# Four places in a two-layer decoder: the order of the first loads, of decay attention's first group, of the last softmax copies and of the last banks

## The chip, the cores and the metric

The kernel runs on one core of a Trainium2 chip. A core has five engines that run side by side and meet at semaphores: TensorE (PE: matmuls, and transposes as matmuls), VectorE (DVE), ScalarE (ACT), GpSimd (POOL) and SyncE (SP), which mostly issues transfers. ACT and POOL can issue transfers as well; SP and ACT have a queue each. Matmuls write to PSUM, which is divided into banks of 128 x 512 float32; DVE and ACT read results from there into SBUF. All other data lies in SBUF or in the chip's memory (HBM).

The metric is the device time of one execution, in microseconds (us); lower is better. Three runs are shown, and their median counts.

## The reference

The input is x, 16 sequences ("blocks" below) of 128 tokens of width 512. Two layers follow, with three sublayers each, and a layer norm behind each addition:

```python
x = _layernorm(x + _L0_attn_ref(x, ...))           # softmax attention, 16 heads, 4 kv heads
x = _layernorm(x + _L0_xattn_ref(x, ctx_512, ...)) # cross attention through latent weights
x = _layernorm(x + _L0_ffn_ref(x, w1, w2, w3))     # gated, ternary weights
x = _layernorm(x + _L1_attn_ref(x, ...))           # decay ("lightning") attention
x = _layernorm(x + _L1_xattn_ref(x, ctx_512, ...)) # softmax attention on the context
x = _layernorm(x + _L1_ffn_ref(x, ...))            # 8 experts, 2 per token, and a shared one
```

The first attention and the fourth sublayer are the ones that the change reaches first:

```python
# _L0_attn_ref
q = q * cos_q + _rotate_half(q) * sin_q
k = k * cos_k + _rotate_half(k) * sin_k
scores = jnp.einsum('btkgd,bskd->bkgts', qg, k) * scale
scores = scores + mask[None, None, None]
p = jax.nn.softmax(scores, axis=-1)
out = jnp.einsum('bkgts,bskd->btkgd', p, v).reshape(B, T, C)
return out @ wo.T + bo

# _L1_attn_ref, in chunks
scores = jnp.einsum('bhid,bhjd->bhij', qb, kb) * intra_decay[None]
o_intra = jnp.einsum('bhij,bhjd->bhid', scores, vb)
...
return out @ Wout + bout
```

The last sublayer adds, for each token, two experts weighted by a softmax gate and a shared expert:

```python
act = jax.nn.silu(gu[..., :F]) * gu[..., F:]
y = jnp.einsum('tef,te,ehf->th', act, combine, down_weights)
sact = jax.nn.silu(sgu[:, :Fs]) * sgu[:, Fs:]
y = y + sact @ shared_down.T
```

Everything is float32.

## The kernel before

All 16 blocks of x stay in SBUF, one tile of 128 tokens x 512 for each. Blocks are worked in four groups of four (`GB` = 4, `NG` = 4): the projections of a group work on 512 tokens at a time. The instructions are written in program order for all engines at once, and a scheduler of the framework then orders each engine's list by what is ready in its model; some instructions are tied to program order (`tc.keep_in_program_order`). Each engine runs its list strictly in order. PSUM's eight banks are shared out by tags (`psum.share`): in softmax attention two are called `mm`, four `sc` and two `pt`; in the last sublayer two `mm`, three `sc`, two `pt` and one `av`.

**The start.** SP's queue loads the rotary tables `rsn` and `rc`, then the weight `w` in five slices (L363) with the small `cols` and `bv` between, then `bo`, `wo` and x4 to x15. ACT's queue loads x0 to x3 (L358) and, after x0, `wv`. POOL multiplies w's halves by the sine table (`t`, L377), DVE multiplies w by the cosine table (L380) and adds the two (`wr`, L381), so that the rotation is in the weight. PE transposes x0 to x3 (L128), works out their values (`pv`, L462) and the 40 matmuls of `pq` (L165), then the first scores (`sc`, L488). POOL adds the output bias `bo` to each block of x (L448) before it comes to the softmax.

**Softmax attention.** `attend` is used by the first attention and by the fifth sublayer. In step n it works out the scores of block n, the values of block n-2 and the output projection of block n-2 (`project_out`, L176). In between, for each of four banks of scores: DVE adds the mask and takes the maximum (L212, L214), ACT takes the exponentials (L219), POOL divides by the sum (`finish`, L226), and `turn` transposes four heads' probabilities on PE into a `pt` bank (L231) and copies them to SBUF on DVE (`pT`, L233). The values (`av`, L494 and L1040) use these copies. A planner (`Share`) deals projections of the next group out over the steps; for block 15 (n = `NB`) in the second use none are left.

**Decay attention.** For each group: eight projections `pq` (L868), then four values `pv` (L878), which DVE copies with their bias to `v` (L883). Then each block goes into a `Pipeline` with lags 0, 1 and 2: its scores on PE (L901, with the decay multiplied in by DVE, `sT`, L908), one step later its values (L916, copied by ACT to `oT`, L921), and one step later its projection (L176). Scores use four `sc` banks, one set. The next group's blocks are transposed through HBM: `send4` copies a block to `xp` on ACT (L144), sends it to HBM (L145) and fetches it turned (L151), and `back` transposes 32 x 32 pieces on DVE (L154). There is one `xp` buffer, and there are two for fetched blocks.

**The end.** Experts' results are added to `sums` in HBM by indirect transfers. Then SP loads the 16 blocks of `sums` (L1392). Half of the shared expert's down projections are still to be done: three pairs of blocks, (8, 12), (9, 13) and (10, 14), by `shared_pair`, with 20 matmuls (L1326, two passes each included) and four short ones (L1334), and blocks 11 and 15 singly by `shared_down`. DVE adds each result to the loaded sum (L1411), in program order. The early blocks 0 to 7 lie between the pairs: POOL adds their sums (L1420). Statistics (L1429), a power on POOL (L1401), ACT's scaling (L1405) and the output transfer (L1408) follow for each.

Of the kernel before, what the change touches and what calls it, by code (L numbers as in the profile page):

```python
# [12 lines left out]
F32 = mybir.dt.float32  # L13
# [5 lines left out]
P = 128  # L19
NB = 16  # L20
D = 512
KC = D // P
# [24 lines left out]
def decoder_kernel(ctx: ExitStack, tc: tile.TileContext, a: dict, out: bass.AP):  # L47
    nc = tc.nc
# [153 lines left out]
    class Softmax:  # L202
# [22 lines left out]
            nc.vector.reciprocal(rs, self.sm)  # L225
            nc.gpsimd.tensor_tensor(self.p, self.p, spread(rs, P), ALU.mult)  # L226

        def turn(self):
            pt = bank("pt", [P, 4, P], "pt")
            for j in range(4):  # L230
                nc.tensor.transpose(pt[:, j, :], self.p[:, j, :], ident)  # L231
            self.pT = self.pool.tile([P, 4, P], F32, tag="pT", name="pT", bufs=4)
            nc.vector.tensor_copy(self.pT, pt)  # L233

    class Share:

# [18 lines left out]
    def attend(pool, mask, wo, prepare, score, value):  # L255


        held = {}
        share = Share(prepare(0), 1)
        share.deal()  # L260
        late = []
        for n in range(NB + 2):
            if n % GB == 0 and n < NB:
                share.rest()
                share = Share(prepare(n // GB + 1), 3 * GB if n + GB < NB else 3 * GB + 6)
            if n < NB:
                sc = [bank("sc", [P, 4, P], "sc") for _ in range(4)]
                score(sc, n)
                held[n] = [Softmax(pool, sc[c], mask) for c in range(4)]
            if n >= 2:  # L270
                av = bank("pt", [P, KC, P], "av")
                value(av, n - 2, [s.pT for s in held.pop(n - 2)])
                oT = pool.tile([P, KC, P], F32, tag="oT", name="oT")
                nc.scalar.copy(oT, av)
            for c in range(4):
                if n < NB:
                    held[n][c].start()
                    late.append(held[n][c])
                if late and (len(late) > 1 or n >= NB):
                    late.pop(0).finish()  # L280
                if 1 <= n <= NB:
                    held[n - 1][c].turn()
                if c == 1 and n >= 2:
                    project_out(oT, wo, n - 2)
                else:
                    share.deal()


    GB = 4
    TG = GB * P  # L290
# [48 lines left out]
    with tc.tile_pool(name="p1", bufs=1) as p1:  # L339
# [9 lines left out]

        with tc.tile_pool(name="p1a", bufs=1, side="right") as p1a:  # L350

            rsn = p1a.tile([P, 640], F32, tag="rsn", name="rsn")
            nc.sync.dma_start(rsn, a["rope_s"].partition_broadcast(P))
            rc = p1a.tile([P, 640], F32, tag="rc", name="rc")
            nc.sync.dma_start(rc, a["rope_c"].partition_broadcast(P))
            w = p1a.tile([P, KC, 640], F32, tag="w", name="w")
            for b in range(GB):
                nc.scalar.dma_start(x[b], a["x"][b])  # L358
                if b == 0:
                    nc.scalar.dma_start(wv, a["l0a_wqkv"][:, :, 640:768])  # L360
            for c in range(5):
                at = slice(c * P, (c + 1) * P)
                nc.sync.dma_start(w[:, :, at], a["l0a_wqkv"][:, :, at])  # L363
                if c == 0:
                    nc.sync.dma_start(cols, a["l0a_cols"])
                    nc.sync.dma_start(bv, a["l0a_bv"].partition_broadcast(P))
            mask1 = load_const("mask1", [P, P], a["mask_add"], p1)
            nc.sync.dma_start(bo, a["l0a_bo"].partition_broadcast(P))
            nc.sync.dma_start(wo, a["l0a_wo"])
            halves = "p (h t d) -> p h t d"  # L370
            for c in range(5):
                at = slice(c * P, (c + 1) * P)
                t1 = p1a.tile([P, KC, 4, 2, 16], F32, tag="t1", name="t1", bufs=2)
                w5 = w[:, :, at].rearrange("p k (h t d) -> p k h t d", t=2, d=16)
                s4 = rsn[:, at].rearrange(halves, t=2, d=16)
                for t in range(2):
                    nc.gpsimd.tensor_tensor(  # L377
                        t1[:, :, :, t, :], w5[:, :, :, 1 - t, :], bc4(s4[:, :, t, :], KC), ALU.mult
                    )
                nc.vector.tensor_tensor(wr[:, :, at], w[:, :, at], bc(rc[:, at], KC), ALU.mult)  # L380
                nc.vector.tensor_tensor(  # L381
                    wr[:, :, at], wr[:, :, at], t1.rearrange("p k h t d -> p k (h t d)"), ALU.add
                )
                if c == 0:
                    nc.vector.tensor_tensor(br, cols[:, 0, :], cols[:, 2, :], ALU.mult)
                    nc.vector.tensor_tensor(b2, cols[:, 1, :], cols[:, 3, :], ALU.mult)
                    nc.vector.tensor_tensor(br, br, b2, ALU.add)
# [423 lines left out]
    with tc.tile_pool(name="p4", bufs=1) as p4:  # L811
# [39 lines left out]
        for g in range(NG):  # L851
# [20 lines left out]
                if c in (2, 4) and g + 1 < NG:  # L872
                    send4((g + 1) * GB + c // 2 - 1)
            vs = []
            for i in range(GB):
                pv = bank("mm", [P, D], "pv")
                for k in range(KC):
                    nc.tensor.matmul(  # L878
                        pv, lhsT=xT[:, k, i * P : (i + 1) * P], rhs=wq4[k // 2][:, k % 2, 2 * D : 3 * D],
                        start=(k == 0), stop=(k == KC - 1),  # L880
                    )
                v = p4.tile([P, D], F32, tag="v", name="v", bufs=6)
                nc.vector.tensor_tensor(v, pv, bv4, ALU.add)  # L883
                vs.append(v)
            if g + 1 < NG:
                xT = p4.tile([P, KC, TG], F32, tag="xT", name="xT")
            for i in range(GB):
                if i in (0, 2) and g + 1 < NG:
                    for n in (i, i + 1):
                        coming.pop(0).back(xT[:, :, n * P : (n + 1) * P])  # L890
                        if i == 0:
                            send4((g + 1) * GB + 2 + n)
                toks = slice(i * P, (i + 1) * P)
                mine = {}

# [26 lines left out]
                    mine["oT"] = oT  # L922

                pipe.push((scores, values, lambda mine=mine, b=g * GB + i: project_out(mine["oT"], wo4, b)))
        pipe.drain()
    pre_pool.__exit__(None, None, None)

# [126 lines left out]
    with tc.tile_pool(name="p6", bufs=1, reuse_waits="tile") as p6:  # L1054
# [173 lines left out]
        with tc.tile_pool(name="p6r", bufs=1, side="right", reuse_waits="tile") as p6r:  # L1228
# [85 lines left out]
                    lambda po: then(b, po),  # L1314
                )

            def shared_pair(tasks, pair, then):


                got = {}  # L1320
# [1 line left out]
                def whole(b, m_):  # L1322
                    g, i = divmod(b, GB)
                    if m_ == 0:
                        got[b] = bank("mm", [P, D], "po")
                    nc.tensor.matmul(  # L1326
                        got[b], lhsT=acts[g][:, m_, i * P : (i + 1) * P], rhs=sw_dn[:, m_, :],
                        start=(m_ == 0), stop=False,
                    )
# [84 lines left out]
            for blocks in order:  # L1414
                tasks = []
                if blocks[0] >= EARLY and len(blocks) == 2:
                    shared_pair(tasks, blocks, add_late)
                for b in blocks:
                    if b < EARLY:
                        tc.keep_in_program_order(nc.gpsimd.tensor_tensor(x[b], x[b], ys[b], ALU.add))  # L1420
# [143 lines left out]
```

## Time and profile before

| what | value |
|---|---|
| median of three runs | 2063.01 us (2058.14 to 2064.41) |
| the profiled execution | 2059.38 us |
| its span, first to last instruction | 2057.5 us |
| granted TensorE clock, mean | 0.992 |
| PE busy | 2006.5 us, 98% |
| DVE, ACT, POOL busy | 886.6, 627.7, 647.5 us |
| HBM read, written | 185.88, 75.83 MB |

A line of a timeline gives the start, the duration, the engine, the line of the kernel, the operation, what it writes from what, the shape and, after x, how many instructions are put together. In brackets behind it stand the idle time of the engine before it and what ended that. A line of the chain of waits gives the start, the duration and the work that the end waited for at that time. The granted clock is a share of full speed.

### The profile page before, as it was taken

What the parts mean: (1) busy time and instruction counts of PE and PEld (TensorE: products, weight loads), DVE (VectorE), ACT (ScalarE), POOL (GpSimd) and SP (SyncE); (2) the same over time, 40 slices, a digit from 0 to 9 for tenths busy, and PEclk for the clock granted to TensorE, in tenths of its full rate; (3) what the DMA queues carried; (4) which work ended last, traced back from release to release, by engine and by line L of the source; (5) the groups of instructions that cost most, each with busy time, mean ns of one, the idle gap of its engine ahead of it and who ended that gap; (6) DMA issues with size and microseconds to landing.
All of it is one profiled execution on the core that took longest, in us unless ns stands there. A gap on an engine that the chain in (4) does not pass through costs nothing.

```text
span 2057.5 us, 25359 instructions
## 1 busy us (share of the span) xinstructions
PE 2006.5 (98%) x9045; PEld 1110.9 (54%) x9045; DVE 886.6 (43%) x1775; ACT 627.7 (31%) x2107; POOL 647.5 (31%) x674
## 2 busy tenths in 40 slices
PE   8999999999999999999999999999899999999997
PEld 4555554444444468888554444555544455555552
DVE  4777732445554354342134414777731123233234
ACT  3555532333333333222311012766522200000002
POOL 7445520211222122223422113455613212323223
PEclk9999999999999999999999999999999999999999
DMA  9201241535432241001410018500013246786844
GB/s 250 87 17 40 104 143 56 158 118 174 149 124 91 71 121 60 16 11 62 147 42 21 11 41 265 203 22 22 27 61 116 95 133 185 226 247 192 264 89 169
DMA packets 164110, 227.87 MB, mean 111 GB/s; under 512 B 50576, under 2 KB 117520, under 8 KB 159248
## 3 DMA queue, kind: packets, MB, share of 16 engines
q1 hardware_dynamic: 149088, 152.80, 23.9%
q0 software_dynamic: 13792, 72.14, 11.6%
q8 instruction: 72, 1.18, 0.2%
q10 hardware_dynamic: 1104, 1.31, 0.2%
q14 instruction: 54, 0.44, 0.1%
HBM read 185.88 MB, written 75.83 MB: 127 GB/s over the span
## 4 chain that ended last, share of the span: by engine, by line
PE 84%; DMA 6%; DVE 3%; POOL 2%; issue 2%; ACT 1%; SPq 0%; POOLq 0%; DVEq 0%; ACTq 0%
PE po L649 10%; PE po L176 7%; PE pq L590 5%; PE pq L868 5%; PE pq L165 5%; PE pg L1143 4%; PE po L799 4%; PE pa L772 4%; PE pb L772 4%; PE pu L1143 3%; DMA sums<-ry,place 3%; PE ry L1292 3%; PE rg L1271 3%; PE ru L1271 3%; PE pv L878 3%; PE av L637 3%
## 5 line engine op out<-in xcount | busy, mean ns | idle before, releaser
L226 POOL TENSOR_TENSOR p<-p,rs 128x512 f32<-128x512 f32 x192 | 201.0, 1048 | 456.9 <-DVE rs L225 447.6
L649 PE MATMUL po<-mT,cc 128*128 128x512 f32 x512 | 230.4, 598 | 1.4 <-ACT cc L642 1.4
L219 ACT ACTIVATE p<-t,nmx 128x128 f32<-128x128 f32 x512 | 198.6, 390 | 33.8 <-POOL p L226 10.2
L649 PEld LDWEIGHTS po<-mT,cc 128*128 128x128 f32 x512 | 94.7, 190 | 115.0 <-issue 106.0
L219 ACT ACTIVATE p<-sc,nmx 128x128 f32<-128x128 f32 x256 | 90.3, 374 | 109.1 <-DVE nmx L214 93.8
L1241 POOL DMA_INDIRECT ew<-in_l1f_w_dram,which x39 | 40.6, 1042 | 246.6 <-PE ry L1292 167.2
L176 PE MATMUL po<-wo,oT 128*128 128x512 f32 x256 | 116.9, 600 | 0.4 <-ACT qkT L454 0.4
L590 PE MATMUL pq<-xT,wqr 128*128 128x512 f32 x256 | 115.8, 593 | 0.9 <-ACT xT L129 0.9
L1276 ACT ACTIVATE rsg<-rg 128x352 f32<-128x352 f32 x39 | 18.1, 464 | 320.6 <-PE rg L1271 297.0
L115 POOL TENSOR_SCALAR ve<-mv 128x1 f32<-128x1 f32 x80 | 17.8, 223 | 301.4 <-DVE mv L113 282.9
L868 PE MATMUL pq<-xT,wq 128*128 128x512 f32 x256 | 110.6, 592 | 0.7 <-ACT xT L129 0.7
L1292 PE MATMUL ry<-ew,ractT 128*128 128x512 f32 (+1 forms) x234 | 106.9, 592 | 0.0
L1271 PE MATMUL rg<-ew,xsT 128*128 128x352 f32 x312 | 100.1, 463 | 6.6 <-DMA ew<-in_l1f_w_dram,which 6.5
L122 POOL TENSOR_SCALAR x<-x,mv,rstd 128x512 f32<-128x512 f32 x48 | 100.5, 2094 | 4.5
L1271 PE MATMUL ru<-ew,xsT 128*128 128x352 f32 x312 | 98.7, 459 | 0.0
L219 ACT ACTIVATION_READ_ACCUMULATOR p<-t,nmx 128x1 f32 x512 | 96.3, 188 | 0.0
L233 DVE COPY pT<-pt 128x512 f32<-128x512 f32 x128 | 86.6, 679 | 19.4 <-PE pt L231 19.4
L783 POOL TENSOR_TENSOR hl<-ht,hh 128x512 fp32r<-128x512 f32 x44 | 57.4, 1305 | 108.1 <-ACT hh L781 108.1
L231 PEld LDWEIGHTS pt<-ident,p 128*128 128x128 f32 x512 | 60.6, 143 | 55.5 <-issue 41.5
L1143 PE MATMUL pg<-xT,sw_gu 128*128 128x512 f32 x192 | 86.5, 593 | 0.0
L1304 POOL DMA_INDIRECT sums<-ry,place x39 | 61.8, 1585 | 70.4 <-DMA sums<-ry,place 34.7
L214 DVE TENSOR_REDUCE nmx<-t 128x4 f32<-128x512 f32 x128 | 83.6, 676 | 0.8
(243 smaller groups left out, 3612.4 us busy)
## 6 DMA issues: line engine op xcount, KB each, us to landing
piece<-in_l0f_w_dram SPq DMA_DIRECT2D x48, 352.0 KB
away<-sq SPq DMA_DIRECT2D x32, 512.0 KB
pT<-away SPq DMA_DIRECT2D x128, 128.0 KB
raw<-in_l0x_raw_dram SPq DMA_DIRECT2D x8, 1728.0 KB
x<-turned SPq DMA_DIRECT2D x176, 64.0 KB
slots_x<-zero SPq DMA_DIRECT2D x1, 10023.0 KB
sums<-zero SPq DMA_DIRECT2D x1, 9984.0 KB
xs<-slots_x SPq DMA_DIRECT2D x156, 64.0 KB
```

The lines of the kernel that those rows point to most:

```text
L122: engine.tensor_scalar(x[b], x[b], mean, rstd, ALU.subtract, ALU.mult)
L165: nc.tensor.matmul(got["p"], lhsT=lhsT, rhs=rhs, start=(n == 0), stop=(n == len(pairs) - 1))
L176: nc.tensor.matmul(po, lhsT=oT[:, c, :], rhs=wo[:, c, :], start=(c == 0), stop=(c == KC - 1))
L219: nc.scalar.activation(self.p[:, j, :], src[:, j, :], AF.Exp, bias=nmx[:, j : j + 1], accum_out=self.sm[:, j : j + 1])
L226: nc.gpsimd.tensor_tensor(self.p, self.p, spread(rs, P), ALU.mult)
L590: nc.tensor.matmul(pq, lhsT=wqr[:, k, cols], rhs=xT[:, k, :], start=(k == 0), stop=(k == KC - 1))
L649: nc.tensor.matmul(self.po, lhsT=self.cc[:, 4 * par + j, :], rhs=mT[h], start=(par == 0 and j == 0), stop=(par == 1 and j == 3),)
L772: nc.tensor.matmul(dst, lhsT=wt[:, k, f * P : (f + 1) * P], rhs=xs[n][:, k, :], start=(k == 0 and n == 0), stop=(k == KC - 1 and n == 1),)
L868: nc.tensor.matmul(pq, lhsT=wq4[k // 2][:, k % 2, c * P : (c + 1) * P], rhs=xT[:, k, :], start=(k == 0), stop=(k == KC - 1))
L1143: nc.tensor.matmul(dst, lhsT=sw_gu[:, k, at : at + P], rhs=xTs[g][:, k, :], start=(k == 0), stop=(k == KC - 1),)
L1271: nc.tensor.matmul(dst, lhsT=self.xT[:, k, :], rhs=gu[:, k, off : off + FE], start=(k == 0), stop=(k == KC - 1),)
L1292: nc.tensor.matmul(po, lhsT=self.actT[:mw, m_, :], rhs=dn[:mw, m_, :], start=(m_ == 0), stop=(m_ == 2))
```

## The change

1. x1 and x3 are loaded by SP, ahead of everything else in its queue; x0, `wv` and x2 stay with ACT.
2. `turn` is told who copies. In step n = `NB` (block 15), in both uses of `attend`, the copies of the second and fourth bank (c = 1, 3) are ACT's; all others stay with DVE.
3. In decay attention's first group, the values and the attention of the blocks are interleaved: after `pv` of block 1, block 0 enters the pipeline, after `pv` of block 2, block 1. Blocks 2 and 3 follow after all four values, and the transposes for the next group (`back`) with the sends of blocks 6 and 7 come ahead of block 2. The other groups keep their order.
4. The pair (9, 13) takes the two `pt` banks in place of the `mm` banks.

The scheduler's order follows: DVE finishes `wr`'s first slice before it starts on the others, POOL makes all ten `t` products before its first addition of `bo`, and SP sends nine blocks in a row (L145) before it fetches blocks 6 and 7, where it sent seven.

```diff
-        def turn(self):
+        def turn(self, copy):
             pt = bank("pt", [P, 4, P], "pt")
...
-            nc.vector.tensor_copy(self.pT, pt)
+            copy(self.pT, pt)
...
-                    held[n - 1][c].turn()
+                    held[n - 1][c].turn(nc.scalar.copy if n == NB and c % 2 else nc.vector.tensor_copy)
...
+            for b in range(1, GB, 2):
+                nc.sync.dma_start(x[b], a["x"][b])
             rsn = p1a.tile([P, 640], F32, tag="rsn", name="rsn")
...
-            for b in range(GB):
+            for b in range(0, GB, 2):
                 nc.scalar.dma_start(x[b], a["x"][b])
...
-            for i in range(GB):
+            def values_in(i):
                 pv = bank("mm", [P, D], "pv")
...
-            if g + 1 < NG:
-                xT = p4.tile([P, KC, TG], F32, tag="xT", name="xT")
-            for i in range(GB):
-                if i in (0, 2) and g + 1 < NG:
-                    for n in (i, i + 1):
-                        coming.pop(0).back(xT[:, :, n * P : (n + 1) * P])
-                        if i == 0:
-                            send4((g + 1) * GB + 2 + n)
+            def attend_block(i):
                 toks = slice(i * P, (i + 1) * P)
...
+            began = 0
+            for i in range(GB):
+                values_in(i)
+                if g == 0 and 0 < i < GB - 1:
+                    attend_block(began)
+                    began += 1
+            if g + 1 < NG:
+                xT = p4.tile([P, KC, TG], F32, tag="xT", name="xT")
+            for i in range(GB):
+                if i in (0, 2) and g + 1 < NG:
+                    for n in (i, i + 1):
+                        coming.pop(0).back(xT[:, :, n * P : (n + 1) * P])
+                        if i == 0:
+                            send4((g + 1) * GB + 2 + n)
+                if i >= began:
+                    attend_block(i)
...
-            def shared_pair(tasks, pair, then):
+            def shared_pair(tasks, pair, then, tag="mm"):
...
-                        got[b] = bank("mm", [P, D], "po")
+                        got[b] = bank(tag, [P, D], "po")
...
-                    shared_pair(tasks, blocks, add_late)
+                    shared_pair(tasks, blocks, add_late, ("mm", "pt")[blocks[0] % 2])
```

## The prediction

> **What bounds the kernel now.** I read the page first, then the chain of waits, then the timeline of TensorE (PE) at the four places that the change touches, then the granted clock there. The page says that PE is busy nearly all the time, so only PE's own idle time, and time at a low clock, can be won:
>
> ```profile
> span 2057.5 us, 25359 instructions
> PE 2006.5 (98%) x9045; PEld 1110.9 (54%) x9045; DVE 886.6 (43%) x1775; ACT 627.7 (31%) x2107; POOL 647.5 (31%) x674
> ```
>
> Place 1, the first 43 us, in the chain of waits (start, duration, what). The reader is to see that GpSimd (POOL) holds PE up: it adds `bo` to 15 blocks, then normalizes the first probabilities, and only then does PE transpose them.
>
> ```profile
> 20.47 2.28 POOL t L377 x2
> 22.75 18.82 POOL x L448 x15
> 41.57 1.01 POOL p L226
> 42.62 0.69 PE pt L231 x2
> ```
>
> Place 2, PE's timeline where decay attention begins, and the same two operations one group later. Between the start of the first scores (1031.45) and the first projection (1043.13) lie 11.68 us; one group later, a score step and a value step follow each other without a wait.
>
> ```profile
> 1031.45 1.17 PE L901 MATMUL sc<-qkT 32*128 32x128 f32 x32
> 1034.09 3.87 PE L901 MATMUL sc<-qkT 32*128 32x128 f32 x32 [1.47 <-DVE sT L908]
> 1037.88 1.94 PE L916 MATMUL av<-sT,v 128*32 128x128 f32 x32
> 1039.75 2.44 PE L901 MATMUL sc<-qkT 32*128 32x128 f32 x32
> ...
> 1093.71 1.17 PE L901 MATMUL sc<-qkT 32*128 32x128 f32 x32
> 1094.81 1.08 PE L916 MATMUL av<-sT,v 128*32 128x128 f32 x32
> ```
>
> Place 3, the last block of the second softmax attention: PE waits for two copies that VectorE (DVE) makes one after the other.
>
> ```profile
> 1478.86 1.04 PE L231 MATMUL pt<-ident,p 128*128 128x128 f32 x8
> 1480.40 0.42 PE L1040 MATMUL av<-pT,v 128*32 128x128 f32 x6 [0.51 <-DVE pT L233]
> 1481.59 1.06 PE L1040 MATMUL av<-pT,v 128*32 128x128 f32 x26 [0.77 <-DVE pT L233]
> ```
>
> Place 4, the end: each late pair of blocks waits for DVE to read the banks of the pair before.
>
> ```profile
> 2010.59 1.13 PE L1334 MATMUL po<-sw_dn,half 64*128 64x512 f32 x4
> 2013.91 10.55 PE L1326 MATMUL po<-sw_dn,act 128*128 128x512 f32 x20 [2.19 <-DVE x L1411]
> ...
> 2026.29 8.85 PE L1326 MATMUL po<-sw_dn,act 128*128 128x512 f32 x20 [0.77 <-DVE x L1411]
> ```
>
> Last the granted clock around places 2 and 4 (window, its length, PE busy with instructions, clock, DMA share, GB/s). A window in which PE was busy 1.93 or 1.21 of 3.40 us is followed by one or two at half clock:
>
> ```profile
> 1031.90:1035.30 3.40, 1.93 (x40) 1.00 0.20 58
> 1035.30:1038.70 3.40, 3.40 (x39) 0.50 0.40 117
> 2011.50:2014.90 3.40, 1.21 (x5) 1.00 0.91 269
> 2014.90:2018.30 3.40, 3.40 (x6) 0.50 1.02 380
> ```
>
> A half-clock window costs about 3.4 / 2 = 1.7 us; the same 20 matmuls took 10.55 behind the 2.19 us gap and 8.85 us otherwise, a difference of 1.70.
>
> [...]
>
> **Tokens first (place 1).** x1 and x3 move from ACT's queue to the head of SP's. The four blocks then come side by side, where PE now waits 2.20 us for the second one (its transposes start at 9.11). PE can start its 40 `pq` matmuls as soon as the last values are done: two transposes of 1.1 us, 16 `pv` matmuls, two transposes, 16 `pv` from 5.82 on give about 14 us instead of 17.05. But what ends last in this stage is POOL: ten `t` products (4.27 + 4.08 + 2.31 = 10.66 us), 16 additions of `bo` (1.26 + 18.82 = 20.1), then `p`. This chain starts when w's first slice lands (POOL starts at 10.27), and that slice now stands behind two more transfers on SP. In the new order DVE finishes the first slice before it begins on the next, so POOL's 0.63 us wait for `wr` between products goes. If w lands as before, `p` starts at 10.27 + 10.66 + 20.1 = 41.0, against 41.57: +0.5 us. PE's 3 us are lost in a longer wait for `p`.
>
> When does w land? SP issues at most four transfers ahead: its fifth (bv) waited until 5.47, its sixth (w's second slice) until 7.90. Now w's first slice is the fifth, and goes when x1 lands, near 5. In the worst case it then takes its 8.48 us again: 5.5 + 8.5 = 14.0, 3.9 us late, a net loss of 3.4. The best case is that POOL does not bind and all 3.0 us count. I take +0.5, because the bytes that must come ahead of w or beside it are the same as before (four blocks, wv, the two tables, w: 2.2 MB), and the two queues together moved 210 to 378 GB/s between 2 and 8 us. Hidden work: x2 still leaves by ACT and, with x4 to x15, is needed later than it lands. PE's longer wait before 42 may cost another half-clock window: -1.7, kept for the range.
>
> [...]
>
> **ScalarE shares the last block's copies.** Two of four copies in each softmax attention move to ACT (128x512 copies from the same kind of bank take ACT 0.59, DVE 0.68 us). Place 3: the last transposes end at 1479.90. DVE does x14's addition, the third copy, a bn_stats and then the fourth copy, which ends at 1481.54. ACT has been idle (8.54 us before its next copy), so the fourth copy ends near 1480.6 and the values near 1481.65 instead of 1482.65: **-1.0 us**, bounds 0 and 1.3 (both waits, 0.51 + 0.77). In the first attention PE ran `pm` matmuls until 250.84 and the values started right then, while DVE's last copy began at 250.27; nothing is won there. On ACT the copy stands ahead of one `mT` copy; PE's next reader of that bank has 0.26 + 0.86 us of other work, so I cost it at nothing, at most 0.6.
>
> **Decay attention beside its values (place 2).** PE's new order in the first group is pv, pv, scores, pv, scores and values, pv, scores and values. While PE does one pv (3.43 us), DVE does four `sT` products (2.44) and one `v` (0.69), so neither scores nor values should wait. Sum: pv 13.73, three scores at 1.10 (1093.71 to 1094.81), two values at 1.01: 19.05 us from 1017.62, so the first projection starts at 1036.7 instead of 1043.13: **-6.5 us**, of which 1.5 is the shown wait, some 3.4 two half-clock windows, and the rest scores held between DVE's products.
>
> What is late next: the transposes of group 1's blocks on DVE (L154) now come after the fourth `v`, near 1036.5 instead of 1033.4, and on SP the fetches of blocks 6 and 7 (4.62 us for eight issues) now stand behind two more sends (L145) and those transposes: about 1036 to 1041, landing near 1043. DVE's x0 addition waits behind block 6's transpose, but PE then has the other bank. Group 1's `pq` needs block 7 and would start at 1046.0 (1052.6 less 6.5). So some 2.5 us are spare; if the fetches land 6 us after their issue, 3 us of the gain are lost. ACT's next oT stands behind two `xp` copies (near 1038.6, needed at 1042.4). POOL's layernorms follow.
>
> **Banks alternate (place 4).** Pair (9, 13) goes to the `pt` banks, free since 2000.5. Then it starts at 2011.7, and pair (10, 14) finds `mm` free since 2014.5. Two pairs at 9.96 us (2026.29 to 2036.25) end at 2031.6; the single block still waits 0.73 for DVE: 2032.35 instead of 2036.98, **-4.6 us** = 2.19 + 0.77 + 1.70 in round figures. Bounds: 2.9 with the clock step paid all the same, 5.0. DVE covers it: it ends block 3's statistics at 2022.6, so it takes up (9, 13) 1 us after PE ends it, before PE needs anything. The last sums land long before: the reads were issued by 2019.4. The tail from the last matmul to the end (9.3 us) stays.
>
> **Sum.** 0.5 + 1.0 + 6.5 + 4.6 = 12.6 us. The profiled execution took 2059.38 us (span 2057.5 and 1.9 around it): 2046.8. It lies 3.6 us below the median of 2063.01, within the runs' spread (2058.14 to 2064.41), so from the median: **2050.4 us**.
>
> **Rivals.**
> Place 1 pays in full (PE's order, not POOL, binds): 3.0 instead of 0.5, 2048. The unbroken run of POOL rows up to 41.57 speaks against it. Chance 0.07.
> Clock steps come back: the half-clock windows are set by short stretches of low activity, and one more at place 1, one kept at place 4 and one elsewhere cost 3 x 1.7: gain 7.5, 2055.5. For it: places with waits of 0.8 to 0.9 us got one too (around 1472). Chance 0.15.
> w lands late and block 7's fetch lands late: 12.6 - 3.9 - 3 = 5.7, 2057.3, within 0.3%. Chance 0.10.
> Slower: SP's order at place 2 turns against it. Each microsecond that block 7's fetch lands after 1046 holds the whole of group 1; from 1058.6 on it eats all 12.6 us, from 1064.8 the kernel is slower by 0.3%, 2069.2 or more. In the trace, the same eight issues ended 4.7 us after their release and nobody waited for them. Chance 0.03.
> The forecast as worked out: 0.65.
>
> 0.3% (6.2 us) is about what a measurement here can tell from no change. Faster by more: 0.65 + 0.07 + 0.15 = 0.87; within: 0.10; slower: 0.03. The range runs from 2044 (place 1 in full, and 3.6 for the spread between runs) to 2057.
>
> **What would show it.** After the change PE's `sc` at the start of decay attention should follow `pv` without a wait on `sT`, and the first projection should start 19 us after the first pv. The second late pair should have no wait on DVE x, and the row of its 20 matmuls should be near 8.9. The last values should be one run of 32. The first `pt` should still wait for POOL's p, near 42. I am wrong if w lands after 12, if DVE's L154 waits for a transfer and `pq` of group 1 for it, or if half-clock windows stand at new places.

## The result and the profile after

| kernel | median, us | lowest to highest | runs |
|---|---|---|---|
| before | 2063.71 | 2058.14 to 2064.67 | 6 |
| after | 2050.68 | 2049.82 to 2054.66 | 6 |

The ratio is 0.9947, 95% interval 0.9937 to 0.9957: 10.9 us faster (8.9 to 13.0). Both medians together would say 13.0; with six runs each that spread over 6.5 and 4.8 us, the interval is the better statement. The same kernel measured again beside other experiments gave 2052.02 us (6 runs) and 0.9943 (0.9921 to 0.9964). The profiled execution took 2050.76 us; its span fell from 2057.5 to 2048.9 us.

The page of the kernel after, first lines. TensorE is as full as before: the same 9045 matmul instructions are 6.0 us less busy time.

```profile
span 2048.9 us, 25361 instructions
PE 2000.5 (98%) x9045; PEld 1105.5 (54%) x9045; DVE 884.0 (43%) x1771; ACT 629.2 (31%) x2111; POOL 647.4 (32%) x674
```

**Place 1.** The chain of waits of the kernel after (start, duration, what). All 16 additions of `bo` now stand in one run behind the products, and the first transposes of probabilities still follow POOL's `p`: 42.35 us, where it was 42.62.

```profile
18.95 2.31 POOL t L380 x2
21.26 20.04 POOL x L451 x16
41.30 1.01 POOL p L226
42.35 0.69 PE pt L231 x2
```

PE's own timeline says where its gain went. Its projections start at 14.75 instead of 17.05; the wait for `p` behind them has grown from 0.61 to 1.83 us, and a scores row from 1.15 to 1.96, since a half-clock window begins in it, at 38.72, and is two intervals of 3.41 us long. (In the profiles before and after, all half-clock windows begin on one grid of 3.41 us; the last section has their starts.) The window is that long, too, in six of the seven profiles whose start is as before; the profile before is the exception.

```profile
14.75 17.33 PE L165 MATMUL pq<-xT,wr 128*128 128x512 f32 x40
...
38.56 1.96 PE L491 MATMUL sc<-qkT 32*128 32x128 f32 x8 [0.23 <-DVE t L212]
42.35 0.69 PE L231 MATMUL pt<-ident,p 128*128 128x128 f32 x2 [1.83 <-POOL p L226]
```

**Place 2.** PE's timeline at the start of decay attention. Nothing in it waits; the first projection starts at 1036.95, 19.56 us after the first `pv`, where it took 25.51. The next group's `pq` follows at 1046.23 without a wait for block 7's fetch.

```profile
1017.39 7.03 PE L882 MATMUL pv<-wq,xT 128*128 128x512 f32 x16
1024.36 1.17 PE L899 MATMUL sc<-qkT 32*128 32x128 f32 x32
1025.46 3.70 PE L882 MATMUL pv<-wq,xT 128*128 128x512 f32 x8
...
1034.83 1.17 PE L899 MATMUL sc<-qkT 32*128 32x128 f32 x32
1035.94 1.08 PE L914 MATMUL av<-sT,v 128*32 128x128 f32 x32
1036.95 3.70 PE L176 MATMUL po<-wo,oT 128*128 128x512 f32 x8
...
1046.23 4.03 PE L871 MATMUL pq<-xT,wq 128*128 128x512 f32 x9
```

**Place 3.** The last values of the second softmax attention, PE's timeline: one run of 32, and of the two waits (0.51 and 0.77) the second is gone.

```profile
1471.47 1.04 PE L231 MATMUL pt<-ident,p 128*128 128x128 f32 x8
1473.01 1.23 PE L1056 MATMUL av<-pT,v 128*32 128x128 f32 x32 [0.51 <-DVE pT L233]
```

**Place 4.** The late pairs follow each other at 9.84 us without a wait; only the single block waits for DVE.

```profile
2006.80 1.13 PE L1350 MATMUL po<-sw_dn,half 64*128 64x512 f32 x4
2007.86 8.85 PE L1342 MATMUL po<-sw_dn,act 128*128 128x512 f32 x20
...
2017.70 8.85 PE L1342 MATMUL po<-sw_dn,act 128*128 128x512 f32 x20
...
2028.38 4.56 PE L165 MATMUL po<-sw_dn,act 128*128 128x512 f32 x10 [0.77 <-DVE x L1427]
```

One thing did not fit: up to the experts the kernel after was 8.4 us ahead of the one before, at the last experts' product only 3.8. That stretch, which the change does not touch, took 350.0 us instead of 345.4. Was this the change's doing, or does the stretch vary by itself? The experiments had to answer that too.

### The profile page after: what moved, and what is told of

Same layout as the page of the kernel before. It is cut to its first block, busy times and chain, and to the rows that moved or that the text cites. A ratio compares the mean times of both kernels' runs of the same rounds, so it can differ in the third digit from the quotient of the medians.

```text
span 2048.9 us, 25361 instructions
## 1 busy us (share of the span) xinstructions
PE 2000.5 (98%) x9045; PEld 1105.5 (54%) x9045; DVE 884.0 (43%) x1771; ACT 629.2 (31%) x2111; POOL 647.4 (32%) x674
## 4 chain that ended last, share of the span: by engine, by line
PE 86%; DMA 5%; DVE 3%; POOL 3%; issue 2%; ACT 1%; SPq 0%; POOLq 0%; ACTq 0%; DVEq 0%
PE po L652 10%; PE po L176 7%; PE pq L593 5%; PE pq L871 5%; PE pq L165 5%; PE pg L1159 4%; PE po L802 4%; PE pa L775 4%; PE pb L775 4%; PE ry L1308 4%; PE rg L1287 3%; PE pu L1159 3%; PE ru L1287 3%; DMA ew<-in_l1f_w_dram,which 3%; PE pv L882 3%; PE av L640 3%
## 5 line engine op out<-in xcount | busy, mean ns | idle before, releaser
L1294 DVE TENSOR_TENSOR ract<-rsg,ru 128x352 f32<-128x352 f32 x39 | 20.3, 521 | 149.9 <-issue 142.8
```

## The experiments

The same marks were read in the trace of every kernel: the first transposes of the cross attention (`pk`, its start), the first `pq` of decay attention, its first `pv` and first `po`, the first `plT` and `rg` of the experts' sublayer, the last `ry` (experts' product) and the last `po`. The table gives the us between them, from one profiled execution each. Two stretches are left out, since they are the same in all (27.57 from `pq` to `pv`, 166.03 from `plT` to `rg`), and so are the last 9.9 us.

| kernel | start | to decay | pv to po | po to plT | experts | tail |
|---|---|---|---|---|---|---|
| before | 258.15 | 731.90 | 25.51 | 448.63 | 345.41 | 44.34 |
| c0_again (before once more) | 258.48 | 732.07 | 25.66 | 448.62 | 347.43 | 42.60 |
| t1_tokens | 260.23 | 732.60 | 25.79 | 448.97 | 350.37 | 44.14 |
| d1_decay | 259.08 | 732.15 | 19.55 | 449.07 | 347.84 | 44.38 |
| s1_copies | 259.45 | 732.64 | 25.79 | 447.95 | 346.82 | 44.33 |
| b1_banks | 258.92 | 732.23 | 25.76 | 448.63 | 352.16 | 39.53 |
| f1_filler | 258.40 | 732.00 | 25.67 | 448.62 | 351.17 | 44.67 |
| f2_filler | 259.15 | 735.07 | 24.27 | 447.45 | 348.83 | 42.62 |
| o0_gpsimd_before | 257.25 | 731.91 | 25.52 | 448.61 | 354.78 | 42.96 |
| after | 257.86 | 731.97 | 19.55 | 446.40 | 350.03 | 39.54 |
| a2_after_again | 259.26 | 732.71 | 19.55 | 447.63 | 348.61 | 39.54 |
| o1_gpsimd | 255.63 | 732.15 | 19.55 | 446.41 | 348.50 | 39.53 |
| o3_gpsimd_again | 255.83 | 731.98 | 19.55 | 446.42 | 350.38 | 39.54 |
| o2_both | 256.55 | 735.10 | 19.55 | 447.92 | 346.39 | 39.53 |

The stretch up to the cross attention can be taken apart further. In all fourteen profiles it is the first `pt` (transposes of probabilities), plus half of the half-clock time behind it, plus a rest: 214.08 to 214.12 us in the eight kernels without the change of the copies, 213.89 to 213.92 in the six with it. So the copies are worth 0.2 us in the first attention, and whatever else differs in that column is the first `pt` and the place of the clock's window.

**The kernel before once more** (no edit).

> The kernel before, unchanged, as a control. Theory: no change, a ratio of 1.000 with an interval inside 0.998 to 1.002. What it tells apart: in the profile before, the last attention half (first rg to last ry, experts' chain) took 345.4 us and in the profile after 350.0 us, although the change does not touch that stretch. If that is the variation of weight transfers from one execution to the next, this second execution of the same code should differ from 345.4 by some microseconds too; if the stretch is as steady as the rest (within 0.5 us of 345.4), the 4.6 us belong to the change.

2064.03 us (12 runs), ratio 1.0006 (0.9996 to 1.0016). Its experts' stretch took 347.4 us, and over all fourteen profiles the stretch lies between 345.4 and 354.8 us, with the change (346.4 to 350.4) and without it (345.4 to 354.8). So the 4.6 us are variation from one execution to the next, in a part whose matmuls wait for the experts' weights. They are no cost of the change, and the profile before was the lowest of all. Two rows of the pages show where they went (busy us, mean ns of one, idle us before, what ended most of it), the kernel before first, then the kernel after:

```profile
L1271 PE MATMUL rg<-ew,xsT 128*128 128x352 f32 x312 | 100.1, 463 | 6.6 <-DMA ew<-in_l1f_w_dram,which 6.5
L1287 PE MATMUL rg<-ew,xsT 128*128 128x352 f32 x312 | 101.9, 470 | 9.2 <-DMA ew<-in_l1f_w_dram,which 8.4
```

2.6 us are longer waits, mostly for the weights `ew`; 1.8 us are slower matmuls, in a half-clock window at 1916.05. Over the fourteen profiles TensorE's waits in this stretch add up to 6.6 to 12.0 us. Two executions of the kernel before differ by up to 10 us (2057.66 to 2068.00 among the 35 of this measurement), so a smaller difference of two spans says little; the other stretches are far steadier.

**Decay attention alone.**

```diff
             for i in range(GB):
+                values_in(i)
+                if g == 0 and 0 < i < GB - 1:
+                    attend_block(began)
+                    began += 1
```

> Only the decay attention beside its values; the other three parts as before. Theory (parts add up, this one is the largest): 6.2 us off the time, ratio 0.9970, the first output projection of the decay attention 6.2 us earlier against its first value matmul (19.6 us instead of 25.5), and no half-clock window there. Rival (the gain is handed back by block 7's transfer or by the experts' weights, and the parts need each other): under 3 us, ratio above 0.9985.

2058.11 us (12 runs), ratio 0.9976 (0.9966 to 0.9987): 5.0 us off (2.7 to 7.0). In the trace the stretch from `pv` to `po` is 19.55 us, to 0.01 us that of the kernel after, against 25.51 to 25.79 in the kernels without this part (f2_filler apart): 6.0 to 6.2 us. The theory holds: no half-clock window stands there, and the next stretch is longer by 0.5 us at most (449.07 against 448.61 to 448.97). The time alone would not quite shut out the rival's 3 us.

**Banks alone.**

```diff
-                    shared_pair(tasks, blocks, add_late)
+                    shared_pair(tasks, blocks, add_late, ("mm", "pt")[blocks[0] % 2])
```

> Only the alternation of banks at the end. Theory: 4.6 to 4.8 us off, ratio 0.9977, the last blocks' pairs of 20 matmuls each at 8.85 us with no wait for VectorE, and no half-clock window near 2015. Rival (the clock window is placed by the free-running grid and comes back elsewhere in the tail): 2.9 us, ratio 0.9986, with one pair still above 10 us.

2060.19 us (12 runs), ratio 0.9986 (0.9975 to 0.9997): 2.9 us off (0.6 to 5.2). That is the rival's number, but the interval holds the theory's 0.9977 as well, and the rival's sign, a pair above 10 us, is missing: all pairs took 8.85 us, and the tail is 39.53 as in the kernel after. But what it is measured against is not one number: without this part the tail takes 44.1 to 44.4 us in four profiles and 42.6 to 43.0 in three, the control among them. The difference is the clock. Below, the granted clock by grid interval (window, its length, then busy time of PE, PEld, DVE, ACT and POOL with instructions, clock, DMA share, GB/s). The gap ahead of the pair (9, 13) is the same (2.19 and 2.15 us). In the kernel before it lies within one interval and leaves PE 1.23 us of work:

```profile
2011.51:2014.93 3.42, 1.23 (x5) 0.54 (x4) 1.76 (x3) 0.00 (x0) 0.00 (x0) 1.00 0.91 272
2014.93:2018.34 3.41, 3.41 (x6) 1.35 (x5) 2.96 (x9) 0.00 (x0) 2.89 (x3) 0.50 1.02 380
```

In its control, c0_again, it is divided between two intervals, and no half clock follows:

```profile
2012.37:2015.79 3.42, 2.01 (x7) 0.42 (x5) 0.00 (x1) 0.00 (x0) 0.00 (x0) 1.00 0.42 147
2015.79:2019.20 3.41, 2.67 (x6) 1.25 (x7) 3.28 (x7) 0.00 (x0) 0.93 (x1) 1.00 0.91 296
```

So the gap cost its 2.2 us in both, and 1.70 more (10.55 against 8.85 us for the pair) only where it left one interval with 1.23 us of work.

**Tokens alone.**

```diff
+            for b in range(1, GB, 2):
+                nc.sync.dma_start(x[b], a["x"][b])
...
-            for b in range(GB):
+            for b in range(0, GB, 2):
                 nc.scalar.dma_start(x[b], a["x"][b])
```

> Only the tokens first on both queues. Theory (GpSimd binds the start: its p copies follow its sums, whatever the tokens do): 0.3 us off, ratio 0.9998, within measurement of no change; TensorE's first pq about 2.3 us earlier and its wait for p 1.2 us longer. Rival (the start pays in full): 2 us or more off, ratio 0.9990 or below.

2063.62 us (12 runs), ratio 1.0004 (0.9992 to 1.0015): nothing that can be measured. The profile's start is even longer (260.23), with the first `pt` at 43.19. PE waits 1.53 us for `p` there, so GpSimd binds here as well; the first `pq` starts only 0.4 us earlier (16.69), since PE's first values waited for `wv` until 9.37 in this execution, and until 8.20 in the profile after. Over all profiles the first `pq` starts at 15.74 to 17.05 in the eight kernels without this part (mean 16.44) and at 14.44 to 16.69 in the six with it (mean 15.33). So the tokens bring TensorE forward by 1.1 us on average; the 2.3 us of the first two profiles took the latest of the eight for comparison. Part of it is that most matmuls of these first values take 417 to 422 ns, and 275 from the point on where the record of the granted clock begins, at 14.72 in the profile before and already at 11.41 in the one after; what the clock was ahead of that point is not shown. GpSimd's first `p` does not move with it: 41.25 to 41.74 without the tokens, 41.26, 41.41 and 42.09 with them, where GpSimd's order is the old one.

**Copies alone.**

```diff
-                    held[n - 1][c].turn()
+                    held[n - 1][c].turn(nc.scalar.copy if n == NB and c % 2 else nc.vector.tensor_copy)
```

> Only ScalarE's share in the copies of the last block's probabilities. Theory: 1.0 us off for the copies at the ends of the two attention turns that show them, and up to 1.2 us more where the half-clock window at 1472.2 goes, so 1.0 to 2.2 us, ratio 0.9990 to 0.9995. Rival (VectorE was not late there, the gain seen in the profile after came from the shifted clock grid): under 0.4 us, ratio above 0.9998.

2064.31 us (12 runs), ratio 0.9997 (0.9985 to 1.0009); a gain of 1 us is too small for this. The traces decide it. s1_copies and t1_tokens have their half-clock windows at the same work (1287.5 and 1288.2, none near 1472), and only the copies differ between them from `po` to `plT`: 447.95 against 448.97, 1.02 us. From the last transposes to the projection it is 3.50 and 4.52 us. Another set of profiles agrees: f2_filler (below) has no half-clock window in that stretch, and neither have after, o1_gpsimd and o3_gpsimd_again; without the copies it takes 447.45 us, with them 446.40 to 446.42. PE's timeline of s1_copies:

```profile
1481.53 1.04 PE L231 MATMUL pt<-ident,p 128*128 128x128 f32 x8
1483.07 1.23 PE L1040 MATMUL av<-pT,v 128*32 128x128 f32 x32 [0.51 <-DVE pT L233]
1485.03 1.55 PE L176 MATMUL po<-wqo,oT 128*128 128x512 f32 x3 [0.73 <-ACT oT L274]
```

And PE's timeline of t1_tokens at the same work, with the second wait:

```profile
1482.25 1.04 PE L231 MATMUL pt<-ident,p 128*128 128x128 f32 x8
1483.79 0.42 PE L1042 MATMUL av<-pT,v 128*32 128x128 f32 x6 [0.51 <-DVE pT L233]
1484.98 1.06 PE L1042 MATMUL av<-pT,v 128*32 128x128 f32 x26 [0.77 <-DVE pT L233]
1486.77 3.70 PE L176 MATMUL po<-wqo,oT 128*128 128x512 f32 x8 [0.73 <-ACT oT L274]
```

**A gap filled at the end** (the kernel before with matmuls that nobody reads).

```diff
+                if blocks[0] == EARLY + 1 and len(blocks) == 2:
+                    spare = bank("sc", [P, D], "spare")
+                    for m_ in range(5):
+                        tc.keep_in_program_order(nc.tensor.matmul(
+                            spare, lhsT=acts[0][:, m_, 0:P], rhs=sw_dn[:, m_, :], start=(m_ == 0), stop=(m_ == 4),
+                        ))
```

> The kernel before with five unused 128x512 matmuls, about 2.1 us of TensorE's time, put into the gap of 2.19 us ahead of the pair of blocks (9,13); they write a bank that nobody reads. The gap itself stays as long as it was, only TensorE is busy in it. Theory (the half-clock window at 2014.9 follows from the gap): the 20 matmuls behind it take 8.85 us as the other pairs do, about 1.7 us off the time, ratio 0.9992. Rival (the window has another cause, or the placing of the grid alone): the window stays, ratio 1.000 or slightly above.

2065.48 us (12 runs), ratio 1.0003 (0.9993 to 1.0013). The experiment missed. Each call became two instructions (10 of `spare` in the trace for 5 calls), so the filler took 4.4 us and not 2.1, twice the gap; the pair started late, and the tail was 44.67, 2.07 us above that of the control. No window stood there, but neither did one in the control. It tells nothing for or against the theory; the two filled gaps further down do.

**GpSimd's order**, on the kernel after and on the one before.

```diff
-                nc.gpsimd.tensor_tensor(x[g * GB + i], x[g * GB + i], bo, ALU.add)
+                tc.keep_in_program_order(nc.gpsimd.tensor_tensor(x[g * GB + i], x[g * GB + i], bo, ALU.add))
```

> The kernel after, with GpSimd's additions of the bias for blocks 8 to 15 moved behind its first p copies; no other engine's order changes. Theory (GpSimd's order binds the start, and the tokens can only pay once it does not): the first pt moves from 42.35 to about 39 us, up to 3.3 us more gain than the change alone, ratio to the kernel before 0.993 against 0.9947. Rival (the start is bound by the weights' transfers that TensorE waits for, and GpSimd is only the last of several): under 0.5 us more, ratio 0.9945 to 0.995.

2049.38 us (6 runs), ratio 0.9927 (0.9909 to 0.9945). GpSimd takes seven additions ahead of `p` instead of 16, and its `p` now waits for DVE, no longer for its own list; PE's first `pt` moved from 42.35 to 40.00 us and waits for nothing. o1_gpsimd, GpSimd's timeline:

```profile
35.06 2.50 POOL L451 TENSOR_TENSOR x<-x,bo 128x512 f32<-128x512 f32 x2 [0.83 <-PE tr L128]
38.36 1.04 POOL L226 TENSOR_TENSOR p<-p,rs 128x512 f32<-128x512 f32 x1 [0.80 <-DVE rs L225]
```

> The kernel before with the same move of GpSimd's additions behind its first p copies. Theory: without the tokens first TensorE itself becomes the bound, so the first pt moves from 42.62 to about 41.2 us only: 1.4 us off, ratio 0.9993. Rival: the move is worth as much without the tokens (3 us, ratio 0.9985), then the order of the tokens has no part in it; or nothing (1.000).

2061.46 us (12 runs), ratio 0.9983 (0.9971 to 0.9995): 3.5 us off (1.0 to 6.0). That is the rival's number (0.9985, the tokens having no part in it), and the theory's 0.9993 lies inside the interval too, so the time does not tell them apart. The traces do, as far as one profile of o0 goes. PE's first `pt`, in o0_gpsimd_before and then in o1_gpsimd:

```profile
41.80 0.69 PE L231 MATMUL pt<-ident,p 128*128 128x128 f32 x2
40.00 0.46 PE L231 MATMUL pt<-ident,p 128*128 128x128 f32 x2
```

It stands at 42.35 to 42.83 in the seven kernels with neither part, at 41.80 with GpSimd's order alone and at 40.00 to 40.29 in the three profiles with both, and in these four it waits for nothing. So the tokens are worth 1.5 to 1.8 us there once GpSimd no longer binds, and nothing before. Of o0's 3.5 us the trace shows 0.8 at this mark; where the rest came from is open.

> The kernel after with GpSimd's additions behind its first p copies once more, since its gain over the kernel after (0.9927 against 0.9947 and 0.9943, in separate measurements) is inside their intervals. Theory (2.2 us or more come from the start, whatever the clock grid does): first pt at 40 to 41 us, cross attention reached by 256.5 us (257.9 and 259.3 in the two profiles after), ratio 0.993 to 0.9937. Rival (the first profile's start was a lucky place on the grid): cross attention at 257.5 us or later, ratio 0.9945.

2052.15 us (5 runs), ratio 0.9934 (0.992 to 0.9947); first `pt` at 40.29, cross attention at 255.83. The start of the three profiles with both parts (o2_both is described below) is 1.3 to 3.6 us shorter than in the two profiles after. Timed, this version stands at 0.9927 and 0.9934 and the kernel after at 0.9947 and 0.9943: the better of the two in the trace's start, but the intervals overlap, so a gain in total time is likely and not shown.

**Two gaps filled in the cross attention**, on the kernel before and on o1.

```diff
+        FILL = {1: 2, 2: 1}
...
+                if m in FILL:
+                    spare = bank("mm", [P, D], "spare")
+                    for n in range(FILL[m]):
+                        tc.keep_in_program_order(nc.tensor.matmul(
+                            spare, lhsT=wkr[:, 0:P], rhs=kvT, start=(n == 0), stop=(n == FILL[m] - 1),
+                        ))
```

> The kernel before with six unused 128x512 matmuls in the two first gaps of TensorE in the cross attention (four in the 2.32 us ahead of the third block's scores, 1.7 us of work at full clock; two in the 1.08 us ahead of the fourth's); they write a bank that nobody reads. All ten profiles so far show a half-clock window of 10.2 to 13.7 us there, behind a grid interval of 3.41 us in which TensorE was busy for 1.1 to 2.0 us. Theory (a grid interval with too little matmul work halves the next one): the window goes or shrinks to one interval, and the stretch from the cross attention's first transposes to the decay attention's first projection falls from 731.9 to 728.5 or less, 3 to 5 us off the time, ratio 0.998. Rival A (the window has another cause): it stays 10.2 us, ratio 1.000 or slightly above. Rival B (the window goes, but ScalarE's exponentials set the pace of the four first blocks): stretch 730.5 to 731.5, under 1.5 us.

2066.59 us (12 runs), ratio 1.0015 (1.0003 to 1.0028): slower. In this stretch the clock did what the theory says. The same stretch by grid interval in the kernel before:

```profile
291.19:294.61 3.42, 1.10 (x12) 0.91 (x10) 1.54 (x4) 2.45 (x15) 0.65 (x1) 1.00 0.47 145
294.61:298.02 3.41, 2.47 (x11) 1.88 (x9) 2.16 (x5) 1.77 (x12) 1.43 (x2) 0.50 0.03 11
298.02:301.43 3.41, 3.16 (x16) 3.17 (x16) 1.92 (x5) 1.77 (x11) 1.81 (x2) 0.50 0.40 159
```

And in f2_filler:

```profile
293.48:296.89 3.41, 2.77 (x16) 1.75 (x16) 1.28 (x4) 2.59 (x16) 1.04 (x1) 1.00 0.54 156
296.89:300.31 3.42, 2.48 (x14) 1.46 (x12) 1.99 (x5) 2.60 (x15) 1.78 (x2) 1.00 0.07 28
300.31:303.72 3.41, 3.17 (x14) 1.64 (x12) 2.50 (x5) 1.80 (x10) 1.34 (x2) 1.00 0.32 129
303.72:307.13 3.41, 1.22 (x4) 0.68 (x4) 1.38 (x5) 2.47 (x10) 2.08 (x2) 1.00 0.80 258
```

The interval ahead went from 1.10 to 2.77 us of matmuls, and three intervals at half clock were gone. The time did not follow, and Rival B's cause is what the trace shows: the fourth block's scores start 40.12 us after the cross attention's first transposes in both, because they wait for ScalarE's exponentials at either clock. PE saved time on the scores and spent it in a new wait of 2.19 us for ACT's `cc`. That left 1.22 us of work in an interval, and the next one was at half clock. PE's timeline of f2_filler:

```profile
301.75 1.98 PE L637 MATMUL av<-pT,kvr 128*128 128x512 f32 x4
305.92 8.83 PE L649 MATMUL po<-mT,cc 128*128 128x512 f32 x16 [2.19 <-ACT cc L642]
```

The whole cross attention, up to the first `pa` of the feed-forward part, took 488.7 us, against 487.7 to 488.5 in the other twelve profiles. Another 2.1 us went between the first `pa` and the decay attention (246.33 against 244.2 in the other twelve, with a half-clock window 3 us behind the first `pa`). It came in both kernels with filler. The fillers take two more tiles of the `mm` ring, which may shift the banks of all that follow; this was not tested, and the cause stays open.

> The kernel after with both additions: GpSimd's additions behind its first p copies, and the six unused matmuls in the cross attention. Theory: 2.2 us from GpSimd's order and 3 to 5 us from the clock, beside the change's own gain: ratio to the kernel before 0.990 to 0.9925, first pt near 40 us, the stretch of the cross and feed-forward part 728.5 or less. Rival (the gains do not add, the weights' transfers in the experts' part take them back): 0.9945.

2051.08 us (6 runs), ratio 0.9935 (0.9914 to 0.9956), not better than o1 alone: the stretch to the decay attention is 735.10 here too. The theory of 3 to 5 us fell.

**The kernel after once more** (no edit).

> The kernel after once more, beside the two others on the same chip. Theory: ratio 0.9945 as measured, its experts' stretch again anywhere between 345 and 355 us, as the eight kernels measured so far spread with no change to it; the other stretches within 0.5 us of the first profile after where no half-clock window falls differently. Rival (the 4.6 us that the profile after lost in the experts' stretch belong to the change): 350 us again.

2052.02 us, 0.9943 (0.9921 to 0.9964); experts 348.6 us. The stretches of places 2 and 4 are the same to 0.01 us. Places 1 and 3 differ by 1.4 and 1.2 us, and both by the clock. At place 1 the window begins 2.67 us later (41.39), so 5.71 us of it lie behind the first `pt` instead of 3.20; half of the difference is 1.25 us, and the first `pt` is 0.16 later. At place 3 a half-clock window stood at 1468.2, where the first profile had none and the kernel before one at 1472.2.

## Why the prediction was right, and where its terms were off

2050.4 us was predicted and 2050.68 measured, 10.9 us off by the ratio where 12.6 had been summed. The agreement to 0.3 us is partly chance, since the medians of before alone went from 2063.0 to 2065.6 between measurements. The terms, by the table of stretches:

| place | predicted | in the traces |
|---|---|---|
| 1, tokens | 0.5 | 0.3 in the first profile, nothing that shows over all |
| 2, decay attention | 6.5 | 6.0 to 6.2 |
| 3, copies | 1.0 | 1.02 to 1.05, and 0.2 in the first attention |
| 4, banks | 4.6 | 3.1 to 4.8, mean 4.1 |

*Place 1* went as reasoned in the main: w landed as before (the products start at 10.08, before at 10.27), GpSimd bound, and PE's earlier start turned into a longer wait. Two steps failed, at little cost. One is "POOL's 0.63 us wait for `wr` between products goes": it stayed, ahead of the fourth slice's products instead of the third's. `p` came at 41.26 against 41.0. The other is "SP issues at most four transfers ahead": w's first slice, the fifth in SP's queue, was issued at 2.60 us and not "near 5", and the sixth waited until 4.63. In all fourteen traces eight transfers of the two queues together were out before the next one waited, four and four before, five of SP and three of ACT after; what sets the eight is not shown. The rival "w lands late" rested on that step. PE's "about 14 us" came at 14.75, although it started 1.07 us earlier than before: its wait of 1.52 us for `wv` is not in that sum.

The tokens alone measured 1.0004, no gain, and the trace shows why: they were earlier (PE's eight first transposes in one run at 4.75 us), and GpSimd's order spent it.

*Place 2*: the order, the missing waits and the two half-clock windows that go were right, and block 7's fetch held nobody. Mis-sized was "one pv (3.43 us)": a `pv` between scores takes 3.63 (1025.46 to 1029.09), and the two in a row 6.97. That makes 19.56 instead of 19.05 us.

*Place 3* was right at 1.02 us. "Nothing is won there", of the first attention, was off by 0.2. What the prediction did not price is the window at 1472. It is there in six of the eight profiles without the copies and in one of the six with them. But in all of these except d1_decay it follows two waits of block 14 (0.91 and 0.84 in the kernel before), whose copies the change leaves alone, so its absence is no gain to count on.

*Place 4*: the waits of 2.19 and 0.77 us went as told. The term that failed is the clock's 1.70 of "2.19 + 0.77 + 1.70", taken as a sure gain. The window stood in four of the seven profiles that have the gap. Their tails took 44.14 to 44.38 us, mean 44.30, and those of the other three 42.60 to 42.96, mean 42.73; by these seven the term is worth 4/7 x 1.57 = 0.9 us on average, an estimate, not 1.7. The rival "Clock steps come back", and with it the sign "half-clock windows stand at new places", came out in part. In the first profile after, place 1's window has a second interval and a new one stands at 1916.05; place 4's is gone. But both kinds stand in kernels without the change as well: two intervals at place 1 in six of seven, windows in the experts' part in b1_banks and o0_gpsimd_before. So no profile shows that the change brings steps back; their places differ between two executions of the same kernel too (at place 1 the window begins at 38.72 in the profile after and at 41.39 in a2_after_again).

Of the other rivals, neither w nor block 7's fetch was late, and SP's sixteen fetches in a row (1036.28 to 1045.11) kept nobody waiting. Parts measured alone sum to 0.24 + 0.14 - 0.04 + 0.03 = 0.37%, each uncertain by 0.1%, against 0.53% for the whole; the stretches add, and nothing shows that a part needed another. Place by place the mean differences of the stretches are 0.1 (two profiles after), 6.1, 1.6 (of which 0.5 is the window of place 3) and 4.1, together 11.9 us.

## What to carry to other kernels

Before a first load is hastened, follow the whole stage to the engine that releases its end: here TensorE was ready earlier, by 1.1 us on average, and GpSimd's list of additions, due much later, took that back; with the list reordered the first `pt` came 2.2 us earlier, though no gain in total time is shown for it beyond the change. Count a gap ahead of TensorE at its length, and the clock step behind it by how often it came (in four of seven profiles here). Judge small parts by steady stretches of the trace, with the same kernel traced twice, for a stage that waits for weights can vary by nearly as much as the whole change is worth (9.4 us here).

## What the runs showed of the hardware

In the profile before, the record of the granted clock begins at 14.72 us, and its half-clock windows at 42.02, 294.61, 1035.30, 1472.21, 2014.93 and 2052.47: whole multiples of 3.4133 us behind the first entry, to within 0.03 us. In the profile after it begins at 11.41, and the windows at 38.72, 294.72, 1916.05 and 2042.35, with the same step and closeness. Their lengths are one, two or three steps, but for the last window of each (7.15 and 8.66 us). The place of this grid differs from execution to execution: an interval begins at 291.19 in the profile before and at 293.48 in f2_filler.

The gap of 2.19 us was followed by half clock in four of seven profiles. The table has full-clock intervals of 3.41 us (start, us of PE busy), by what followed them:

| run | half clock followed | full clock followed |
|---|---|---|
| before | 38.60, 2.92; 291.19, 1.10; 1031.89, 1.94; 1468.80, 1.66; 2011.51, 1.23 | 1479.03, 2.13 |
| after | 1912.63, 1.50 | |
| d1_decay | 2009.80, 1.19 | |
| f2_filler | 303.72, 1.22; 747.48, 1.92 | 293.48, 2.77; 2017.17, 1.50 |
| c0_again | | 2012.37, 2.01 |
| o0_gpsimd_before | | 2020.81, 1.53 |

Half clock followed all four with 1.10 to 1.23 us of work, but no amount of work divides the rest: it followed 1.50 us in the profile after and not in f2_filler, and it followed 1.66, 1.92, 1.94 and 2.92 us, but not 1.53, 2.01 or 2.13. A fuller interval did not end half clock at once either: in the rows of the kernel before, 3.16 us busy at 298.02 was followed by another half-clock interval, since that window is 10.24 us long from 294.61 on. So busy time alone is not what the clock went by here; what else it went by is not shown.

Work that nobody needs kept the clock up (2.77 us busy instead of 1.10) and still made the kernel 0.15% slower, since the scores had been waiting for ScalarE at either clock. Of a half-clock window only that part cost time here which no wait for another engine hid: in the start, where PE's wait for `p` ends with the first `pt`, half of the part behind it in all fourteen profiles (3.20 us of window behind the first `pt` in the profile after, 5.71 in a2_after_again: 1.25 us later).
